# Three pairs instead of four take the plain layer 0 at the front of a four-layer graph network

## The chip, the core and the metric

The kernel runs on one core of a Trainium2 chip. The core has five engines with a queue of instructions each: TensorE (PE in the profile) multiplies matrices into PSUM, VectorE (DVE) and ScalarE (ACT) work on PSUM and SBUF, GpSimd (POOL) on SBUF alone, and SyncE (SP) issues the transfers between the device's memory and SBUF. [...] The metric is the device time of one execution in microseconds; less is better.

## The reference

The input x holds 128 graphs of 64 nodes with 512 features, all with one 64x64 adjacency matrix. Four layers follow, and each ends in `x = layernorm(x + layer(x))`:

- Layer 0: `deg * (x Wi^T + b) + adj (x Wj^T)`, with Wi and Wj the halves of one 512x1024 weight. The kernel applies the graph first, since the graph works on nodes and the weight on features: it forms deg*x and adj*x and multiplies both by their half, 1024 features into 512.
- Layer 1: graph attention with four heads of 512x512, elu, an output attention with a 2048x512 weight, elu, a feed-forward part of two 512x512 weights with relu, and a layernorm of its own with gamma and beta.
- Layers 2 and 3: graph attention with one 512x512 weight each.

All is float32.

## The kernel before

**Tiling.** Two graphs fill the 128 partitions of a tile; two tiles (T = 2) are a pair, of 256 rows. There are NP = 32 pairs, and each goes through the stages `stage_first` (layer 0), `stage_scores` and `stage_heads` (layer 1's attention and its heads), `stage_project` (the output weight), and `stage_late` (output attention, feed-forward, layers 2 and 3). The last pair has `stage_last` and `stage_tile` in place of `stage_late`.

**Two forms of layer 0.** Both begin with the aggregation: PE multiplies x by `aggr` into `axp`, ACT copies that to `ax`, and POOL adds the bias times the degree, `degb`, to x (lines 896 to 912). After that, pairs p >= AHEAD go through `strassen` (line 685): the product of 2x2 blocks is made from seven block products instead of eight. POOL makes sums of `ax` blocks (tiles `s2`, `s3`; in the profile `s`), and the weight's blocks and their differences come ready made from the device's memory, seven parts of 512 KB for every pair (`part_from`, line 613; `ws_w` and `ws_w_T` in the profile, through a ring of four buffers that the output weight's parts share). The products go to the PSUM tiles `stx` and `sty`, and DVE adds them to x. Pairs p < AHEAD take plain products instead, at the front of the program, since the prepared parts are not there yet (lines 914 to 926):

```python
if p < AHEAD:
    ps = psum.tile([P, D], FP, tag="b", name=f"l0_{p}_{t}")
    for k in range(KC):
        with nc.together():
            for s in range(2):
                nc.tensor.matmul(
                    ps, lhsT=ax[:, s, t, k, :], rhs=w0[s][:, k, :],
                    ...
```

A plain tile has eight matmuls of 512 columns. Its PSUM tile is `l` in the profile, where each float32 matmul shows as two records. The last factor of the aggregation also depends on AHEAD (line 905): for Strassen the second tile's `aggr` holds the sum of two blocks.

**The weight's place.** The plain weight `w0` has no buffers of its own. Line 448 puts its halves into the two buffers of the tag `ys`, and `stage_scores` writes its aggregated rows `y` to the same tag (line 976):

```python
w0 = [unit.tile([P, KC, D], FP, tag="ys", bufs=2, name=f"w0_{s}") for s in range(2)]
y = unit.tile([P, KC, 2, T, P], FP, tag="ys", bufs=2, name=f"ys_{p}_{q}")
```

**The front.** The x of pairs below AHEAD is loaded before the weights of the heads (line 541). Then DVE takes 32 dot products of head weights with attention vectors (`score_weights`, line 508, tile `wa_h`). Pairs 0 and 1 get their attention scores from PE: transposes `x1Tp`, products `fp`, then on DVE `over`, on PE `bc`, on DVE a chain of softmax steps that ends in `e`, on PE the transposes `pt`, on ACT the copies `aT`, on PE the aggregation `yp`, and on ACT the copies to `ys`. From `ys` the first head products `sty_h` and `stx_h` start. Other pairs get their scores from DVE's dots with rows of weights (`rows<-d_h`), after which PE turns them (`f2p`). `stage_stream` (line 580) loads every other weight in blocks, has POOL form the differences and stores all to the device's memory, from which `part_from` reads.

**The order.** The stages are generators. A queue in time units (`start`, lines 1303 to 1340; a turn, TURN, is 107) says in which sequence they note their steps: a pair p < AHEAD starts its layer 0 at 0.2 p - 1.2 turns, every other pair at p - 1.1 turns; the scores of p start at p - 0.5, its projection at p + 0.6, its late stage at p + 1.42. The number of a step in that sequence is its rank. `play` (line 327) adds to the rank a shift by kind of step, from the table LATER. A kind is the engine's two first letters and the name of the tile that is written, `te:hidp` for PE's `hidp`. The suffix /S holds for the first 11% of the steps, /E for the last 7%:

```python
when = "S" if i < 0.11 * n else "E" if i > 0.93 * n else "M"
s.rank += LATER.get(s.kind, 0) + LATER.get(f"{s.kind}/{when}", 0)
```

`order` (line 229) then plays the program through with assumed durations (`cost`, line 353). Whenever an engine is free, it takes the ready step of the lowest rank. A step that follows another engine's is ready WAIT + SLACK later, and SLACK for steps behind PE is 0.8. The engines' queues hold the steps in the order found, so every instruction of the program carries the line of the call in `play`, 336. Names of tiles, and not lines, tell the groups of the profile apart.

Of the kernel before, what the change touches and what calls it, by code (L numbers as in the profile page):

```python
# [28 lines left out]
NWS = 4  # L29
NWK = 6  # L30
UNITS = 3
AHEAD = 4

# [4 lines left out]

WAIT = 0.152
NEAR = 150
SLACK = {"tensor": 0.8, "sync": 0.4}

LATER = {
    "gp:never/S": -100, "gp:rs_i": -60, "gp:s_o/S": -20, "gp:ys/E": -40, "sc:aT": -100,
    "sc:aTg/S": 20, "sc:elu/S": -40, "sc:hT": 120, "sc:oT": 60, "sc:who": -80, "sc:xT": -200,  # L50
    "sc:xT/S": -180, "sc:ys/S": 132, "sy:beta/S": -12, "sy:raw_w": 180, "te:fp/S": -20,
    "te:hidp/E": -40, "te:hidp/S": 28, "te:l": 29, "te:l/S": 69, "te:pt": -28, "te:pt/E": 200,
    "ve:e": -29, "ve:e/S": 40, "ve:f_o/S": -120, "ve:hT": 100, "ve:has": 200, "ve:mv": -100,
    "ve:mv/E": 100, "ve:mx": -20, "ve:o": -140, "ve:r": -40, "ve:r/E": 40, "ve:sh": 10,
    "ve:sm": -80, "ve:st": -13,
}


# [105 lines left out]
class Plan:  # L164
# [64 lines left out]
    def order(self):  # L229
# [21 lines left out]
        def late(s, e):  # L251
            return 0.0 if s.engine == e else WAIT + SLACK.get(s.engine, 0.3)

# [120 lines left out]
def gnn_stack_kernel(  # L374
# [43 lines left out]
    def load_x(p):  # L418
        t = xp.tile([P, T, D], FP, tag="x", name=f"x_{p}")
        nc.sync.dma_start(out=t, in_=x[ts(p, T * P), :].rearrange("(t p) d -> p t d", p=P))  # L420
        return t
# [118 lines left out]

    for p in range(1, AHEAD):
        xs[p] = load_x(p)
# [344 lines left out]
    def stage_first(p):  # L887

        if p not in xs:
            xs[p] = load_x(p)  # L890
            yield 0.3 * TURN

        ax = unit.tile([P, 2, T, KC, P], FP, tag="ax", name=f"ax_{p}")
        for t in range(T):
            x = xs[p][:, t, :]
            ps = [
                psum.tile([P, KC, 2, N], FP, tag="b", name=f"axp_{p}_{t}_{b}")
                for b in range(2)
            ]
            with nc.together():  # L900
                for c in range(KC):
                    for b in range(2):
                        nc.tensor.matmul(
                            ps[b][:, c, :, :], lhsT=x[ts(b, N), ts(c, P)],
                            rhs=aggr[ts(b, N), 0 if p < AHEAD else t, :, :], start=True, stop=True,
                        )
            with nc.soon():
                for b in range(2):
                    nc.scalar.copy(
                        ax[:, :, t, :, ts(b, N)], ps[b].rearrange("p c s i -> p s c i")  # L910
                    )
            nc.gpsimd.tensor_tensor(x, x, degb, ALU.add)
            yield 3.0
# [7 lines that stand above are left out]
                                start=(k == 0 and s == 0), stop=(k == KC - 1 and s == 1),  # L921
                            )
                    if k == 1:
                        yield 4.0
                nc.vector.tensor_tensor(x, ps, x, ALU.add)
                normalize(x, f"0_{p}_{t}")
                yield 4.0
        if p >= AHEAD:
            A = lambda k, t: ax[:, k, t, :, :]
            yield from strassen(  # L930
                A, part_from("w0", p), sums(A, KC, nc.gpsimd), xs[p], KC, f"0_{p}", 3.0,
                whole=lambda t: normalize(xs[p][:, t, :], f"0_{p}_{t}"),
            )
        first.add(p)
        yield 0.0
# [367 lines left out]
    def start(at, order, stage):  # L1303
        heapq.heappush(queue, (at, order, stage))

    for p in range(NP):
        if p < AHEAD:
            start(TURN * (0.2 * p - 1.2), 10 * p + 4, stage_first(p))
# [84 lines left out]
```

## Time and profile before

| | us |
|---|---|
| median of three runs | 3310.98 (3309.94 to 3311.04) |
| the profiled execution | 3313.95 |
| its span, first to last instruction | 3312.2 |
| PE busy | 3265.2 (99%) |
| DVE busy | 2374.4 (72%) |
| POOL busy | 1724.0 (52%) |
| ACT busy | 1364.6 (41%) |
| mean granted clock of TensorE | 0.994 |
| DMA | 726.08 MB, 219 GB/s |

The profile shows one execution. Busy time adds up an engine's instructions; PE's are pipelined, so a record lasts longer than the distance to the next. The granted clock is the share of TensorE's full clock that the chip gave it in a stretch. A group of the profile reads "line engine operation, tile written <- tiles read, forms, count", and a bracket or a last column gives the idle time ahead of it with the instruction that ended it. The timeline counts from the start of the span.

### The profile page before, as it was taken

The page shows a single profiled execution, that of the slowest core. Times are in us where ns is not written, and L with a number is a line of the kernel's source. Part 1 is how long each engine was busy: PE and PEld are TensorE (multiplying, and loading weights), DVE is VectorE, ACT ScalarE, POOL GpSimd, SP SyncE. Part 2 cuts the span into 40 slices and gives each one's busy share as a digit, 9 for nine tenths or more (in the row PEclk, how much of TensorE's full clock was granted, in tenths as well). Part 3 has the DMA queues.
Part 4 walks back from the last instruction along what each step waited for, and adds up shares of the span by engine and source line. Part 5 has one row for each costly group of instructions (what it writes and reads, how often), then busy time and mean ns, then how long its engine had stood idle before and what let it go on. Part 6 is the DMA issues. An engine that isn't in the chain of part 4 may idle for free.

```text
span 3312.2 us, 60000 instructions
## 1 busy us (share of the span) xinstructions
PE 3265.2 (99%) x21268; PEld 2881.8 (87%) x21268; DVE 2374.4 (72%) x5668; ACT 1364.6 (41%) x3226; POOL 1724.0 (52%) x1860
## 2 busy tenths in 40 slices
PE   8999999999999999999999999999999999999997
PEld 4888888898988989989889988888889899898885
DVE  5467767777777777777777777777777767777766
ACT  2434344343444434444443443434444344343442
POOL 6745445554555555455454555645554455554442
PEclk9999999999999999999999999999999999999998
DMA  8956666767667676667766667676666766667652
GB/s 303 338 177 215 221 203 215 234 208 237 211 210 233 213 247 197 200 230 221 242 204 220 212 217 236 214 226 208 214 233 208 246 201 202 229 216 238 227 183 77
DMA packets 306584, 726.08 MB, mean 219 GB/s; under 512 B 34240, under 2 KB 43504, under 8 KB 306288
## 3 DMA queue, kind: packets, MB, share of 16 engines
q1 hardware_dynamic: 306288, 722.26, 67.1%
q8 instruction: 171, 2.80, 0.3%
q14 instruction: 125, 1.02, 0.1%
HBM read 688.69 MB, written 33.44 MB: 218 GB/s over the span
## 4 chain that ended last, share of the span: by engine, by line
PE 91%; DVE 4%; DMA 3%; POOL 1%; issue 1%; ACT 0%; SPq 0%; POOLq 0%; DVEq 0%; ACTq 0%
PE stx_h L336 13%; PE stx_o L336 13%; PE stx L336 12%; PE sty_h L336 10%; PE sty_o L336 9%; PE sty L336 9%; PE hidp L336 7%; PE yp L336 4%; PE gp L336 3%; PE stx_y L336 3%; PE sty_y L336 2%; PE axp L336 2%; PE l L336 1%; PE op L336 1%; PE oTp L336 1%; DMA d_f<-f 1%
## 5 line engine op out<-in xcount | busy, mean ns | idle before, releaser
L336 DVE CUSTOM_DVE_ANT_0 j<-x,rows 128x512 bf16<-128x512 f32 x736 | 584.1, 794 | 94.3 <-DMA rows<-d_h 75.6
L336 PE MATMUL stx_h<-ys,wh 128*128 128x128 f32 x3072 | 403.8, 275 | 0.7 <-DVE hT L336 0.7
L336 PEld LDWEIGHTS stx_h<-ys,wh 128*128 128x128 f32 x3072 | 381.1, 192 | 22.3 <-DVE sh L336 5.7
L336 POOL TENSOR_SCALAR rs<-mv 128x1 f32<-128x1 f32 x256 | 104.1, 407 | 406.2 <-DVE mv L336 392.2
L336 ACT COPY hT<-stx_h 128x256 f32<-128x256 f32 x384 | 143.0, 372 | 384.6 <-PE stx_h L336 378.6
L336 ACT ACTIVATE x<-x,sh,rs 128x512 f32<-128x512 f32 x256 | 207.2, 813 | 223.6 <-DVE sh L336 221.0
L336 PE MATMUL sty_h<-ys,wh 128*128 128x128 f32 x2048 | 273.8, 277 | 0.0
L336 PEld LDWEIGHTS sty_h<-ys,wh 128*128 128x128 f32 x2048 | 254.4, 192 | 9.0 <-issue 0.5
L336 PE MATMUL stx_o<-ws_wo_T,s_o 128*128 128x256 f32 x1024 | 246.0, 383 | 0.5 <-ACT who L336 0.5
L336 DVE TENSOR_TENSOR x<-stx,x 128x256 f32<-128x256 f32 x360 | 150.8, 420 | 132.1 <-PE stx L336 131.0
L336 PE MATMUL sty_o<-ws_wo,hT 128*128 128x256 f32 x1024 | 243.2, 380 | 0.1
L336 PE MATMUL hidp<-oT,w 128*128 128x256 f32 (+1 forms) x1056 | 228.9, 373 | 0.0
L336 PEld LDWEIGHTS hidp<-oT,w 128*128 128x128 f32 x1056 | 194.0, 190 | 24.9 <-ACT oT L336 0.2
L336 PEld LDWEIGHTS stx_o<-ws_wo_T,s_o 128*128 128x128 f32 x1024 | 190.2, 191 | 28.4 <-ACT who L336 2.1
L336 PEld LDWEIGHTS sty_o<-ws_wo,hT 128*128 128x128 f32 x1024 | 190.8, 191 | 25.6 <-issue 1.1
L336 DVE SCALAR_TENSOR_TENSOR hT<-elu,hT 128x512 f32<-128x512 f32 x256 | 174.9, 684 | 43.3 <-ACT elu L336 41.3
L336 POOL TENSOR_TENSOR ys<-ys,t 128x256 f32<-128x256 f32 x128 | 102.9, 814 | 189.8 <-PE sty_h L336 189.4
L336 ACT ACTIVATE elu<-hT 128x512 f32<-128x512 f32 x256 | 153.0, 599 | 108.7 <-DVE hT L336 104.6
L336 POOL TENSOR_TENSOR rs<-rs,mhalf 128x1 f32<-128x1 f32 x256 | 173.4, 677 | 21.1
L336 DVE BATCH_NORM_STATS2 st<-x 128x6 f32<-128x512 f32 x256 | 176.5, 689 | 5.1
L336 DVE TENSOR_TENSOR hT<-sty_h,hT 128x256 f32<-128x256 f32 x256 | 107.2, 420 | 81.2 <-PE sty_h L336 69.3
L336 ACT COPY ys<-yp 128x512 f32<-128x512 f32 x256 | 132.2, 602 | 78.4 <-PE yp L336 71.7
(205 smaller groups left out, 7629.3 us busy)
## 6 DMA issues: line engine op xcount, KB each, us to landing
ws_wo_T<-d_wo_T SPq DMA_DIRECT2D x256, 512.0 KB, 3.9
ws_wo<-d_wo SPq DMA_DIRECT2D x192, 512.0 KB, 5.3
ws_W_T<-d_W_T SPq DMA_DIRECT2D x248, 256.0 KB, 4.2
rows<-d_h SPq DMA_DIRECT2D x240, 256.0 KB, 4.7
ws_w_T<-d_w_T SPq DMA_DIRECT2D x112, 512.0 KB, 4.9
ws_W<-d_W SPq DMA_DIRECT2D x186, 256.0 KB, 4.1
ws_w<-d_w SPq DMA_DIRECT2D x84, 512.0 KB, 5.2
rows<-d SPq DMA_DIRECT2D x128, 256.0 KB, 4.3
```

The costliest lines, as they stand in the source:

```text
L336: getattr(getattr(self.tc.nc, s.engine), name)(*map(real, args), **{k: real(v) for k, v in kw.items()})
```

## The change

AHEAD goes from 4 to 3. Pair 3 thus loses its place at the front: its x is not loaded ahead of the head weights, its aggregation uses the other `aggr` for the second tile, its layer 0 starts at 1.9 turns instead of -0.6, and it is made by `strassen` with streamed parts instead of by plain products. The table LATER is replaced by another, and SLACK behind PE goes from 0.8 to 0.799. No other line changes.

```diff
-AHEAD = 4
+AHEAD = 3
...
-SLACK = {"tensor": 0.8, "sync": 0.4}
+SLACK = {"tensor": 0.799, "sync": 0.4}
...
 LATER = {
-    "gp:never/S": -100, "gp:rs_i": -60, "gp:s_o/S": -20, "gp:ys/E": -40, "sc:aT": -100,
-    "sc:aTg/S": 20, "sc:elu/S": -40, "sc:hT": 120, "sc:oT": 60, "sc:who": -80, "sc:xT": -200,
-    "sc:xT/S": -180, "sc:ys/S": 132, "sy:beta/S": -12, "sy:raw_w": 180, "te:fp/S": -20,
-    "te:hidp/E": -40, "te:hidp/S": 28, "te:l": 29, "te:l/S": 69, "te:pt": -28, "te:pt/E": 200,
-    "ve:e": -29, "ve:e/S": 40, "ve:f_o/S": -120, "ve:hT": 100, "ve:has": 200, "ve:mv": -100,
-    "ve:mv/E": 100, "ve:mx": -20, "ve:o": -140, "ve:r": -40, "ve:r/E": 40, "ve:sh": 10,
-    "ve:sm": -80, "ve:st": -13,
+    "gp:gT/S": -200, "gp:hid": 60, "gp:hid/S": 80, "gp:ident": -80, "gp:mhalf": -60,
+    "gp:raw_W": 20, "gp:raw_w/S": -40, "gp:raw_wo/S": -40, "gp:ys/E": -60, "sc:aT": -280,
+    "sc:elu/S": -180, "sc:o": 20, "sc:o/S": -40, "sc:who": -100, "sc:ys/S": 140,
+    "te:bc/E": -120, "te:bc/S": 120, "te:fp/S": -120, "te:hidp": -3, "te:hidp/E": 34,
+    "te:hidp/S": 120, "te:l": 40, "te:l/S": 51, "te:pt": -28, "te:pt/E": 220, "te:stx_o/S": -36,
+    "te:sty/E": -60, "te:sty_y": -40, "te:sty_y/S": 80, "te:xTp/S": 60, "ve:e": -160,
+    "ve:f_o/S": -120, "ve:hT": 200, "ve:has": 360, "ve:mv": -160, "ve:o": -360, "ve:r": -180,
+    "ve:sh": 10, "ve:sm": -80, "ve:st": -13,
 }
```

## The prediction

> **What bounds the kernel now.** I read the page first: busy shares, then the slices.
>
> ```profile
> PE 3265.2 (99%) x21268; PEld 2881.8 (87%) x21268; DVE 2374.4 (72%) x5668; ACT 1364.6 (41%) x3226; POOL 1724.0 (52%) x1860
> ...
> PE   8999999999999999999999999999999999999997
> ```
>
> TensorE (PE) is the bound; only the first and last slice fall below nine tenths. Next, busy time by stretches, cut where the timeline of PE changes character (columns: stretch, length, busy us of PE, its weight loads, DVE, ACT, POOL, then granted clock, DMA share, GB/s).
>
> ```profile
> 14.20:68.00 53.80, 51.87 (x220) 26.61 (x218) 34.95 (x87) 13.68 (x25) 37.08 (x35) 1.00 0.89 314
> 68.00:92.00 24.00, 23.32 (x123) 13.77 (x124) 11.69 (x19) 9.82 (x23) 18.39 (x15) 0.93 0.94 337
> ...
> 180.00:232.00 52.00, 46.37 (x248) 37.86 (x247) 33.35 (x78) 17.47 (x42) 17.22 (x19) 0.90 0.72 226
> 232.00:330.00 98.00, 96.74 (x681) 87.11 (x681) 72.45 (x169) 43.05 (x106) 60.33 (x61) 1.00 0.59 186
> 330.00:3200.00 2870.00, 2864.01 (x18920) 2565.40 (x18919) 2099.73 (x4993) 1203.34 (x2848) 1489.75 (x1611) 1.00 0.68 220
> ...
> 3240.00:3312.00 72.00, 52.28 (x184) 33.87 (x183) 44.76 (x136) 20.34 (x58) 16.90 (x32) 0.83 0.20 62
> ```
>
> From 330 to 3200 us PE idles 6 us of 2870: there only less PE work helps. What an order can win lies in 180 to 232 (5.6 idle, clock 0.90) and after 3240. Third, the timeline of PE (start, length, what; brackets: idle before it, and what ended that).
>
> ```profile
> 68.68 1.03 PE L336 MATMUL x1Tp<-ident,x 128*128 128x128 f32 x4 [1.99 <-ACT ax L336]
> 69.51 8.38 PE L336 MATMUL l<-w,ax 128*128 128x512 f32 x16
> 77.73 0.60 PE L336 MATMUL pt<-ident,e 128*128 128x128 f32 x4
> 78.17 3.60 PE L336 MATMUL l<-w,ax 128*128 128x512 f32 x8
> 81.60 1.85 PE L336 MATMUL fp<-wa_h,x1T 128*128 128x8 f32 x16
> 83.38 2.95 PE L336 MATMUL yp<-aT,x 64*128 64x128 f32 x48
> 86.26 3.70 PE L336 MATMUL l<-w,ax 128*128 128x512 f32 x8
> ...
> 91.94 1.05 PE L336 MATMUL sty_h<-ys,wh 128*128 128x128 f32 x8
> ```
>
> `l` is the plain product, 16 records a tile, 128 in all. These last 32 are two tiles, by their number and place pair 3's; the first head product follows at 91.94. The timeline of ACT shows what they hold up:
>
> ```profile
> 89.14 4.01 ACT L336 COPY ys<-yp 128x512 f32<-128x512 f32 x8 [4.72 <-PE l L336]
> ```
>
> The two `ys` buffers held the plain weights w0. The copy of the finished `yp` waits 4.72 us for an `l`, the last reader of w0. So the heads start only when every front pair's plain product is done.
>
> **What the Trainium skill says.** "TensorE: Matmul & The Clock Gate", Part 1, says that PE falls to half clock after an idle window of about 3.4 us and returns after a busy one. The trace agrees on rate and length: 68.8 to 72.2, 184.9 to 191.7 and 225.8 to 229.2 us each show a granted clock of 0.50. It differs on the trigger: gaps of 1.99 and 2.53 us precede the first and third. So an idle gap here costs itself plus about 1.7 us for each such window. The same page, Back-to-back issue gap, prices 512 columns at 216 ns. Here eight `l` records take 3.43 us (78.17 to 81.60), 429 ns each, and 256 columns 216: the measurement decides. "SBUF — State Buffer", SBUF: two separate sides, calls the port pair of VectorE and GpSimd an exclusive lock; the trace agrees (a 128x1 `sh` took 2.29 us at 65.02 beside a long POOL subtraction, 0.15 at 25.73).
>
> **The change part by part.**
> *PE work.* Out: 32 records of 429 ns, 13.7 us. In: seven products of four matmuls, two records each, 56 x 216 ns = 12.1. The aggregation `axp` stays (two groups of 1.16, 2.3 us), so pair 3's layer 0 later costs 14.4. Saving alone: 1.6.
> *The front.* Removed are pair 3's `axp` (2.3, the sixteens at 46 and 52 us) and the `l` stretches 8.2, 3.4 and 3.6: 17.6 us, a half-clock loss of 1.7 among them. That shortens the time to the first head only as far as the attention chain of pair 0 follows. I walk that chain. Scores end at 61.6, `over` at 63.0. `bc` runs at 65.23 behind eight `l` of pair 2 (2.1 lost); `e` starts 2.7 later than `bc` allows, because DVE does pair 2's `sh`, add and statistics; `e` is finished at 74.9, but `pt` waits for the sixteen `l` until 77.7 (2.7); `yp` runs at 83.4 where `aT` was there at 80.4 (3.0); the `ys` copies start at 89.1 where the first `yp` groups were done by 84.7 (4.4). The last three, 10.1, are pair 3's and go. The load of x_3 (512 KB) leaves a queue at 390 GB/s ahead of W_heads: 1.3 us. Sum 11.4. The first two (4.8) are pair 2's and depend on the new places; I take half. So the first head comes 13.8 earlier, 78.1 us, against 14.4 paid later: **+0.6**. Bounds: only the `ys` wait goes, 4.4, giving +10.0; all 17.6 goes, giving -3.2.
> *92 to 330 us.* Bracketed idle there: 1.50+1.06+0.70+1.55+0.29+0.46+2.53+0.37+0.89 = 9.35. The half-clock windows 184.9 to 191.7 and 225.8 to 229.2 hold 9.7 us of busy PE, half lost: 4.9. Together 14.2. The waits are on `hT`, `e_1o`, `aT_1o`, `who`: latencies of few chains, with no layer-0 product in sight. Pair 4's `axp` comes at 301.9, its products at 332 to 358. Pair 3's come a turn (104 us) earlier, about 198 to 254, inside this stretch, and `ve:e`, `ve:r`, `ve:o`, `sc:aT` move the very steps that PE waits for ahead. I take half: **-7.1** (bounds -14.2, and +3 for one new gap with its window).
> *Tail.* Brackets from 3200 on add to 15.9, half clock to 8.0 (16.0 busy in three windows), PE's last record ends 7 before the span: 31. In the last seven per cent of the steps `ve:mv` goes from 0 to -160, `ve:r` from 0 to -180, both on the serial chain of norms and attentions; `te:hidp` from -40 to +31. I take 5%: **-1.5** (bounds -9 and +9).
> *At nothing.* Pair 3's extra DVE: one 128x512 add of 0.69 and five of 0.42 for two of 0.69, +1.4; POOL: three `s`/`ax` sums of 1.27, +3.8; the weight loads of PE, 56 for 32 at 190 ns. They hide beneath PE (in 180 to 232 DVE is 64% busy, POOL 33%); uncovered, 5.2 together. Pair 3's `degb` adds, `rs`, `ax` copies and normalization leave a front where POOL is 77% busy (18.4 of 24) for one that is emptier: no price, it is in the chain above. DMA: x_3 moves on SP behind the stream stores, and seven w0 parts of 512 KB join, 3.7 MB or 17 us at 220 GB/s, with a DMA share of 0.6 to 0.7 around them. Each takes one of the four `ws` buffers, which the `wo` parts use, so its issue waits on SP for their last reader. Behind it stand the `rows` of pair 2's and 3's scores, on which DVE's dots wait 4.0 us between 180 and 232 already; PE sees that only if `f2p` of pair 3 (290.4 before, 36 after pair 3's products) gets late. The w0 stream's stores are issued by 127, some 70 before use. SLACK 0.799 and the other places have 6 us of idle to work on between 330 and 3200: 0 (-2 to +3).
> *Sum.* +0.6-7.1-1.5 = -8.0. Against the profiled execution (3313.95, span 3312.2, 1.75 around it): 3305.9. Its median of runs lies 2.97 lower, at 3310.98: **3303 us**.
>
> **The rivals.**
> *The front chain becomes the bound (slower).* Place: fp to the first head, 60 to 92 us. DVE is the reason: 32 score dots end at 57.9 whatever pair 3 does, and PE would have only pair 1's transposes as cover. If just the 4.4 is gained, the front is +10.0, and PE idle for over 10 us runs the next 6.8 at half clock, +3.4: 3324. It decides once the first head comes after 84.1 (a gain under 7.8) with nothing won later. For it: POOL is 18.4 of 24 busy there and stretches DVE. Against: the three waits counted away are visibly `l`'s.
> *The gaps only move (same).* Starved chains at 180 to 232 come earlier with the heads and keep their latencies; pair 3's products arrive after them. Then +0.6 and the tail zero: 3311.6. For it: the waits are latencies, not missing work.
> *The tail opens (slower).* Two more gaps like the one of 3.49 us at 3283 with windows of 6.8, 2 x (3.5+3.4) = 13.8, less half of the gain in the middle and the rest: 3319.
> That pair 3 is pulled to the front again is excluded: its parts are stored too late.
>
> **How the numbers follow.** Chances: forecast 0.48 (own range 3294 to 3304), same 0.17, front chain 0.27, tail 0.08. A difference of 0.2%, 6.6 us, is about what a measurement of this kernel can tell from no change; so faster 0.48, same 0.17, slower 0.35. The low end is +0.6 in front, the whole 14.2 of the middle and 3 of the tail, 3294; 0.05 lies below. The high end of 3322 is a front of +11; some 0.13 of the front rival and 0.02 of the tail lie above.
>
> **What would show it.** No `l` after about 75 us and 96 in all; 56 more `stx`/`sty` with `ax`; the first `sty_h` near 78 (after 84: the front rival); bracketed idle of PE from there to 330 at half of 9.4 and one half-clock window fewer; span from 3200 to the end of the same shape less 1 or 2 us. Wrong if idle between the last `l` and the first head exceeds 8 us, or if the tail's idle grows past 20.

## The result, and the profile after

The changed kernel takes 3316.12 us (median of 15 runs, 3312.87 to 3321.87) against 3310.29 (15 runs, 3304.11 to 3316.41) of the kernel before beside it: a ratio of 1.0016 with a 95% interval of 1.0009 to 1.0022. It is slower by 0.16%, some 5 us, where 8 us less were forecast. Its profiled execution took 3314.58 us with a span of 3312.8, 0.6 longer than the span before; a second profile of it has a span of 3318.3. The profiled execution of the kernel before, 3313.95, lies 3.7 above its median, so the first pair of profiles shows less of a difference than the medians do.

The page after, busy shares and slices:

```profile
PE 3260.1 (98%) x21292; PEld 2887.1 (87%) x21292; DVE 2393.4 (72%) x5672; ACT 1361.8 (41%) x3226; POOL 1726.1 (52%) x1863
...
PE   7999999999999999999999999999999999999997
```

PE is busy for 5 us less, but its first slice has gone from 8 to 7. The same stretches as before (length, busy us of PE, its weight loads, DVE, ACT, POOL; granted clock, DMA share, GB/s):

```profile
14.20:68.00 53.80, 47.90 (x187) 24.46 (x187) 33.07 (x87) 14.25 (x27) 36.11 (x32) 1.00 0.95 344
68.00:92.00 24.00, 16.73 (x125) 14.66 (x126) 13.03 (x19) 9.36 (x21) 19.50 (x16) 0.64 1.01 371
...
180.00:232.00 52.00, 51.49 (x336) 45.32 (x334) 30.33 (x61) 18.20 (x40) 30.12 (x31) 0.95 0.64 198
232.00:330.00 98.00, 97.28 (x619) 86.15 (x619) 71.45 (x176) 39.34 (x93) 42.78 (x51) 1.00 0.71 226
330.00:3200.00 2870.00, 2864.76 (x18963) 2569.24 (x18962) 2123.43 (x4995) 1201.67 (x2855) 1498.72 (x1618) 1.00 0.68 220
3240.00:3312.00 72.00, 51.70 (x190) 32.94 (x190) 44.64 (x136) 20.84 (x59) 17.05 (x32) 0.85 0.21 62
```

Between 180 and 232 us PE's idle time went from 5.6 to 0.5 and its clock from 0.90 to 0.95: the gain in the middle came. But between 68 and 92 PE now idles 7.3 instead of 0.7, at a clock of 0.64 instead of 0.93. The timeline of PE there:

```profile
56.56 1.85 PE L337 MATMUL fp<-wa_h,x1T 128*128 128x8 f32 x16
58.26 3.68 PE L337 MATMUL l<-w,ax 128*128 128x512 f32 x8
...
62.76 1.02 PE L337 MATMUL bc<-over,bones 128*128 128x512 f32 x2
68.16 3.16 PE L337 MATMUL fp<-wa_h,x1T 128*128 128x8 f32 x16 [4.38 <-ACT x1T L337]
77.59 2.08 PE L337 MATMUL bc<-over,bones 128*128 128x512 f32 x2 [6.27 <-DVE over L337]
...
81.36 6.31 PE L337 MATMUL yp<-aT,x 64*128 64x128 f32 x64 [0.84 <-ACT aT L337]
87.59 1.16 PE L337 MATMUL sty_h<-ys,wh 128*128 128x128 f32 x8
```

The plain products end at 61.9. `bc` of pair 0 runs soon after, at 62.76, and from there PE has only the attention chain: it idles 4.38 and 6.27, and the second `fp` and `bc` run at half clock (3.16 and 2.08 us for 1.85 and 1.02). The first head product comes at 87.59, 4.3 earlier than before and 9.5 later than forecast. The timeline of DVE shows where pair 0's softmax stands:

```profile
63.43 0.18 DVE L337 BATCH_NORM_AGGREGATE mv<-st 128x2 f32<-128x6 f32 x1
71.43 0.69 DVE L337 TENSOR_TENSOR e<-bc,f 128x512 f32<-128x512 f32 x1 [7.81 <-PE fp L337]
72.04 0.55 DVE L337 SCALAR_TENSOR_TENSOR sh<-mv,rs 128x1 f32<-128x1 f32 x1
...
76.35 1.18 DVE L337 TENSOR_TENSOR over<-f,ident 128x512 f32<-128x512 f32 x1
```

Its inputs `bc` and `f` are there by 63.8, yet `e` waits 7.81 us for the `fp` of the next pair. What it waits for is not data but a buffer: pair 1's transposed rows `x1T` lie in the buffers of the tags `dg` and `e`, and `fp`, which ends at 71.3, is their last reader. The timeline of ACT shows why that `fp` is late in turn:

```profile
63.82 0.25 ACT L337 COPY wat_h<-wap_h 32x128 f32<-32x128 f32 x1 [0.22 <-PE bc L337]
67.53 0.58 ACT L337 COPY x1T<-x1Tp 128x512 f32<-128x512 f32 x1 [3.45 <-DMA d_h<-wat_h]
```

The other `x1T` takes the buffer of `dg`, in which `wat_h` lies until its store has landed. In the kernel before, pair 1's `x1T` came at 74.1 and 78.4, after pair 0's first `e`. These lines of its timelines of DVE and ACT show the order:

```profile
68.77 0.66 DVE L336 TENSOR_TENSOR e<-bc,f 128x512 f32<-128x512 f32 x1
...
74.09 0.56 ACT L336 COPY x1T<-x1Tp 128x512 f32<-128x512 f32 x1
```

**An account by stretches.** For the runs below I price every record of PE at its mean distance to the next between 400 and 3050 us (`l`, which does not occur there, at 429 ns), and call what a stretch takes beyond the sum its loss: idle time, half clock and late starts together. "Head" is the first `sty_h`. The first 14 us (losses of 3.0 to 4.7) and the 5 before PE's first record are left out. The two profiles of the changed kernel, after and after_again, differ by up to 2.4 in a column, so single differences of that size say nothing.

| | head at | loss 14 to head | head to 180 | 180 to 330 | 330 to 3000 | 3000 to 3200 | 3200 to end |
|---|---|---|---|---|---|---|---|
| before | 91.9 | 6.4 | 3.9 | 13.2 | 2.8 | -1.0 | 34.1 |
| after | 87.6 | 18.6 | 6.9 | 2.6 | -3.6 | 3.2 | 34.4 |
| after_again | 89.1 | 19.9 | 5.0 | 4.8 | -1.6 | 2.6 | 36.8 |
| e1_ahead_only | 85.4 | 15.7 | 9.9 | 10.5 | 0.4 | 6.5 | 36.1 |
| e2_places_only | 103.0 | 19.2 | 6.3 | 11.0 | 13.9 | 0.1 | 33.5 |
| e3_own_buffers | 79.5 | 10.6 | 18.7 | 5.5 | 0.5 | 3.4 | 34.7 |
| e3b_own_buffers_before | 90.0 | 4.9 | 6.6 | 11.1 | 4.4 | -0.6 | 32.9 |
| e6_own_late | 81.4 | 11.4 | 14.8 | 12.0 | 2.8 | 2.9 | 35.3 |
| e7_late_before | 90.1 | 4.4 | 13.4 | 17.0 | 1.1 | -0.7 | 32.0 |
| e8_cover | 90.8 | 10.8 | 7.2 | 5.7 | 17.5 | 3.4 | 34.4 |
| e9_same_order_own | 88.4 | 19.2 | 5.7 | 4.3 | -0.1 | 2.6 | 32.8 |
| e10_pair4_early | 90.5 | 4.6 | 4.8 | 8.8 | 7.8 | 8.3 | 32.6 |
| e11_rs_first | 86.6 | 18.0 | 7.8 | 3.8 | 0.0 | 3.0 | 32.4 |
| e12_rs_first_own | 82.1 | 13.7 | 10.7 | 1.4 | -1.1 | 3.7 | 35.3 |

The sum of the prices is 3243.7 with four pairs in front and 3242.3 with three, 3256.0 for e8_cover. So of before against after: work -1.4, front +12.2, head to 330 us -7.6, the long middle -6.4, the stretch before 3200 +4.2, tail +0.3, the first 14 us -0.4. They add to 0.9, rounding included, where the spans differ by 0.6.

### The profile page after: what moved, and what is told of

The parts are those of the page before. It is cut to its first block, busy times and chain, and to the rows that moved or that the text cites. A ratio compares the mean times of both kernels' runs of the same rounds, so it can differ in the third digit from the quotient of the medians.

```text
span 3312.8 us, 60061 instructions
## 1 busy us (share of the span) xinstructions
PE 3260.1 (98%) x21292; PEld 2887.1 (87%) x21292; DVE 2393.4 (72%) x5672; ACT 1361.8 (41%) x3226; POOL 1726.1 (52%) x1863
## 3 DMA queue, kind: packets, MB, share of 16 engines
q14 instruction: 125, 1.02, 0.1%
## 4 chain that ended last, share of the span: by engine, by line
PE 91%; DMA 4%; DVE 2%; POOL 1%; SPq 1%; issue 1%; ACT 0%; POOLq 0%; DVEq 0%; ACTq 0%
PE stx_o L337 13%; PE stx_h L337 13%; PE stx L337 12%; PE sty_h L337 10%; PE sty_o L337 10%; PE sty L337 9%; PE hidp L337 6%; PE yp L337 4%; PE gp L337 3%; PE stx_y L337 3%; PE sty_y L337 2%; PE axp L337 2%; PE op L337 1%; PE oTp L337 1%; SPq L337 1%
## 5 line engine op out<-in xcount | busy, mean ns | idle before, releaser
L337 POOL TENSOR_TENSOR s<-gT 128x256 f32<-128x256 f32 x62 | 49.5, 798 | 270.3 <-DVE gT L337 258.4
L337 ACT COPY ax<-axp 128x512 f32<-128x512 f32 x128 | 68.5, 589 | 281.6 <-PE axp L337 277.8
```

Source lines behind the costliest of these rows:

```text
L337: getattr(getattr(self.tc.nc, s.engine), name)(*map(real, args), **{k: real(v) for k, v in kw.items()})
```

## The experiments

Each was run beside the kernel before on the same chip.

**The two parts alone.** e1_ahead_only is the kernel before with

```diff
-AHEAD = 4
+AHEAD = 3
```

> AHEAD = 3 alone; table LATER and SLACK as before. Loss is the time of a stretch less PE's records in it, priced at their distances in the steady part: from 14 us to the first head product 6.4 before and 18.6 after, from there to 330 us 17.2 before and 9.5 after. Theory A (with three pairs in front, pair 1's transposed rows get the buffers 'e' and 'dg' ahead of pair 0's softmax, whatever the places): front loss 15 to 20, first head at 85 to 90 us. Theory C (the new places delay pair 0): front loss under 10, first head at 76 to 80. For the middle: if pair 3's seven-product layer 0 is the filler, loss to 330 us under 11; if the new places did it, about 17. A time of 3312 to 3320 under A with the filler, 3308 to 3312 under C.

e2_places_only keeps `AHEAD = 4` and takes the new LATER and SLACK:

> The new LATER and SLACK 0.799 alone; AHEAD stays 4. Theory A: front loss as before, 6 to 9, first head at 91 to 94 us. Theory C: front loss 15 or more, first head after 97. Middle: filler theory 15 to 19 of loss to 330 us, places theory about 9. A time of 3308 to 3314 under A with the filler theory, 3302 to 3306 under A with the places theory, 3318 or more under C.

Measured: 3332.39 us against 3307.93, a ratio of 1.0073 (1.006 to 1.0087), and 3344.31, 1.011 (1.0096 to 1.0124). Each part alone is worse than both together, and neither has the gain in the middle: head to 330 us loses 20.4 and 17.3, before 17.1, after 9.5. Two parts that cost 0.7% and 1.1% alone cost 0.16% together, so the places and the number of pairs can't be priced apart. Both times lie far above what was expected under theory A. In front, e2 gives the figures of theory C: with four pairs there, the new places alone delay pair 0, at waits on `ax` and `e`. e1 gives those of theory A, but not its mechanism: pair 1's `fp` is through at 66.9, before pair 0's `bc` ends at 68.9, so the shared buffer holds nothing up there. What e1 does have is the hole of the changed kernel ahead of pair 1's `bc`, whose `over` stands behind pair 0's softmax in DVE's queue; this hole needs no new places:

```profile
75.79 2.08 PE L336 MATMUL bc<-over,bones 128*128 128x512 f32 x2 [6.88 <-DVE over L336]
```

**The shared buffers.** e3_own_buffers is the changed kernel, e3b_own_buffers_before the kernel before, with

```diff
-xT = unit.tile([P, KC, P], FP, tag=("dg", "e")[t], name=f"x1T_{p}_{t}")
+xT = unit.tile([P, KC, P], FP, tag="s3", bufs=2, name=f"x1T_{p}_{t}")
```

> The changed kernel, with the transposed rows x1T of pairs 0 and 1 in the two buffers of tag s3, which stand empty then, instead of 'dg' and 'e'. Theory A: DVE's e of pair 0 no longer waits for fp of pair 1, and x1T no longer for the landing of d_h; first head at 79 to 82 us instead of 87.6, front loss 9 to 13, half clock there at most 7 us instead of 17.1; time 6 to 9 under the changed kernel's, 3307 to 3310. Theory B (the chain of scores and softmax is that long by itself): first head at 86 to 88, time as the changed kernel's, 3314 to 3318.

> The kernel before with the same move of x1T to s3: a control. There pair 0's softmax had the buffer first, and PE is covered by pair 3's plain products. Theory A and B: no change, first head within 1.5 us of 91.9, time within 3 us of before. More than 4 us faster would say that the shared buffers cost the kernel before as well.

Measured: 3328.94 against 3307.93, 1.0068 (1.0055 to 1.0081), and 3311.21, 1.0009 (1.0002 to 1.0015). In e3 the first head comes at 79.5, as early as I had forecast for the change, and the loss ahead of it falls by 8.0. But by the ratios the whole is 0.3 to 0.5% slower than the changed kernel (1.0016 in one set of runs, 1.0037 in another), where a gain of 6 to 9 us was expected. The control comes out 3 us slower, at the edge of what was expected. The timeline of PE shows where the next idle time stands:

```profile
121.26 3.35 PE L337 MATMUL sty_o<-ws_wo,hT 128*128 128x256 f32 x8 [5.91 <-DMA ws_wo<-d_wo]
132.25 1.99 PE L337 MATMUL sty_o<-ws_wo_T,hT 128*128 128x256 f32 x8 [2.52 <-DMA ws_wo_T<-d_wo_T]
...
183.31 0.44 PE L337 MATMUL pt_1o<-ident,e_1o 128*128 128x128 f32 x1 [5.05 <-DVE e_1o L337]
```

The heads are done earlier, and the output weight's parts are not: they are issued at 117.4 in this run and land after. Head to 180 loses 18.7. But with the new buffers the planner found another order, so this run alone can't separate the two.

**That gate moved.** e6_own_late is e3 with the stream that prepares w0 later, e7_late_before the kernel before with the same edit:

```diff
-start(0.6 * TURN, 0, stage_stream(W0T, "w0"))
+start(1.2 * TURN, 0, stage_stream(W0T, "w0"))
```

> x1T in the buffers s3 as in e3_own_buffers, and the stream that prepares w0 noted at 1.2 turns instead of 0.6, so that it no longer goes through the four ws buffers ahead of pair 0's output weights. Ring theory (in e3 the 8 us won in front were lost again where sty_o waited 5.9 and 2.5 us for ws_wo, because the w0 stream held the ring): ws_wo is issued before 110 us instead of 117.4, the loss from the first head to 180 us falls from 18.7 to under 9, first head still at 79 to 81; time 8 to 15 under e3's 3328.9, 3314 to 3321. Bandwidth theory (the transfers are simply not done by then): ws_wo lands no earlier than 118 us, loss 15 to 20, time 3324 to 3332.

> The kernel before with the w0 stream at 1.2 turns instead of 0.6, nothing else. Its chain of waits runs through that stream to stx_o at 134 us. Ring theory: ws_wo issued before 115 us instead of 124.4, the waits of 1.5 and 1.1 us at 126.6 and 133.1 go, loss from the first head to 180 us 1 to 3 instead of 3.9; time 3305 to 3310, since little is idle there. Bandwidth theory: no change, 3308 to 3313. More than 6 us slower would say that the stream at its new place delays something later.

Measured: 3332.36 against 3306.13, 1.0074 (1.0061 to 1.0086), and 3325.2, 1.0055 (1.0043 to 1.0067). Both times missed. The edit costs the kernel before as well (head to 330 loses 30.4 for 17.1). In e6 the first part `ws_wo` is issued at 97.8, before the 110 expected, and PE's wait at 121 us is gone; but up to 180 us it still loses 14.8, where under 9 was expected, since its timeline has two other waits:

```profile
156.62 3.75 PE L337 MATMUL stx_o<-ws_wo_T,s_o 128*128 128x256 f32 x8 [8.57 <-POOL s_o L337]
188.38 0.45 PE L337 MATMUL pt_1o<-ident,e_1o 128*128 128x128 f32 x1 [6.13 <-DVE e_1o L337]
```

The idle time has moved and not gone. As each of these orders was found anew, they don't show that the new waits stood behind the old one all along.

**More cover.** e8_cover is the changed kernel with a plain product's worth of needless work for each tile of pair 2, 13.7 us of PE in all:

```diff
+if p == AHEAD - 1:
+    ps = psum.tile([P, D], FP, tag="b", name=f"l0_{p}_{t + T}")
+    for k in range(KC):
+        with nc.together():
+            for s in range(2):
+                nc.tensor.matmul(
+                    ps, lhsT=ax[:, s, t, k, :], rhs=w1_sb[:, k, :],
+                    ...
```

> The changed kernel with 16 needless plain products in front, as many as pair 3's were: layer 0 of pair 2 multiplies its aggregation by w1 into two PSUM tiles that nobody reads. It adds 13.7 us of PE work and leaves nothing out. Cover theory (the front waits on other engines and pair 3's plain products stood there for nothing): the first head comes at 87 to 93 us all the same, front loss falls from 18.6 to 5 to 10 with the needless work counted as work, time 0 to +5 on the changed kernel. Work theory (PE work is what the front costs): first head at 98 to 102 us, time +10 to +14.

Beside it the changed kernel ran again:

> The changed kernel unaltered, on the chip of the three runs below: 3 to 7 us over the kernel before. Front loss (14 us to the first head product, time less priced PE work) 18 to 19, first head at 87 to 88 us, as in its first profile, if these are the program's and not one execution's.

Measured: 3345.83 and 3319.74 against 3306.13, ratios of 1.0121 (1.0108 to 1.0134) and 1.0037 (1.0023 to 1.005). The first head comes at 90.8, where 87.6 and 89.1 stood without the needless work: 13.7 us more of PE's work moved it by 2 to 3, and the loss ahead of it fell from 18.6 and 19.9 to 10.8. That fits the cover theory, but it doesn't show that the chain takes its time anyway, since the chain isn't the same. PE's timeline of e8:

```profile
75.54 1.02 PE L337 MATMUL bc<-over,bones 128*128 128x512 f32 x2
...
90.81 1.16 PE L337 MATMUL sty_h<-ys,wh 128*128 128x128 f32 x8
```

The new order has the needless products ahead of pair 0's `bc`, which runs 12.8 later than in the changed kernel. From there to the head it takes 15.3 us instead of 24.8, for in this order pair 1's `x1T` come after pair 0's `e`, and pair 2's `sh` are done before it. The late start and the shorter chain nearly cancel. The time as a whole missed: with the order found anew, 17.5 us of loss appeared between 330 and 3000, far from the edit.

**The same order.** To be rid of that, e9_same_order_own plans with the old buffers and makes the real tiles with the new ones. Each engine's order is that of the changed kernel:

```diff
-self.made = self.pool.real.tile(self.shape, self.dtype, **self.args)
+args = self.args
+if args.get("name", "").startswith("x1T_"):
+    args = {**args, "tag": "s3", "bufs": 2}
+self.made = self.pool.real.tile(self.shape, self.dtype, **args)
```

> The changed kernel with every engine's instructions in the very same order (the order is found as before, and only the buffers that x1T of pairs 0 and 1 really get are changed, from 'dg' and 'e' to s3). So nothing is planned anew. Theory A1 (the shared buffers alone are the loss in front, and what is won there stays won): first head at 79 to 82 us, time 6 to 9 under the changed kernel, which ran at 3319.7 beside a kernel before at 3306.1, so 5 to 8 over the kernel before. Theory A2 (behind that gate stands a second, the prepared output weights at 121 us, so idle of PE moves there and is not removed): first head at 79 to 82, loss from 14 us to the first head 9 to 12 instead of 18.6 to 19.9, loss from there to 180 us 11 to 15 instead of 5 to 7, time within 3 us of the changed kernel. Theory B (the chain itself is that long): first head at 86 to 89.

Measured: 3316.54 (3312.89 to 3321.92) against 3311.32, 1.0019 (1.001 to 1.0028), the changed kernel's time; the first head at 88.4, where theory B had it. The buffer's wait is gone and nothing is gained, but not because the chain itself is that long. The timeline of DVE says why:

```profile
64.26 0.69 DVE L340 TENSOR_TENSOR e<-bc,f 128x512 f32<-128x512 f32 x1 [0.21 <-PE bc L340]
71.56 0.16 DVE L340 SCALAR_TENSOR_TENSOR sh<-mv,rs 128x1 f32<-128x1 f32 x1 [6.60 <-POOL rs L340]
71.63 0.69 DVE L340 SCALAR_TENSOR_TENSOR bc<-e 128x512 f32<-128x512 f32 x1
```

`e` starts 7.2 us earlier. Next in DVE's queue is pair 2's `sh`, which waits 6.60 for `rs`, and pair 0's softmax stands behind it. The timeline of POOL of the same run has `rs` behind three long subtractions for the output weight:

```profile
63.50 7.18 POOL L340 TENSOR_TENSOR raw_wo<-raw_wo,raw_wo 128x1024 f32<-128x1024 f32 x3
70.65 0.22 POOL L340 TENSOR_SCALAR rs<-mv 128x1 f32<-128x1 f32 x1
```

In the changed kernel the two `rs` (each of two records) stand behind the same subtractions and end at 70.5 and 71.3, about when the buffer comes free (71.3). Its POOL timeline:

```profile
62.49 7.18 POOL L337 TENSOR_TENSOR raw_wo<-raw_wo,raw_wo 128x1024 f32<-128x1024 f32 x3
...
70.78 0.56 POOL L337 TENSOR_TENSOR rs<-rs,mhalf 128x1 f32<-128x1 f32 x1
```

So two gates of nearly one length stand side by side, of which the waits named only one. In the kernel before, POOL's timeline has the first of them ahead of those subtractions:

```profile
64.11 0.22 POOL L336 TENSOR_SCALAR rs<-mv 128x1 f32<-128x1 f32 x1
...
64.95 4.79 POOL L336 TENSOR_TENSOR raw_wo<-raw_wo,raw_wo 128x1024 f32<-128x1024 f32 x2
```

The new LATER ranks `raw_wo` 40 earlier at the start (`gp:raw_wo/S`), which the old one doesn't. With the old table e1 too has an `rs` ahead of the three subtractions and one between them (62.9 and 66.1); with the new one e2 too runs the three in a row. That may point to this entry, but no run changes it alone.

**Both gates.** e11_rs_first keeps the changed kernel's order and buffers, but takes the `rs` steps of pair 2 forward in POOL's queue: those of the first tile ahead of all three subtractions and three `wh` differences before them, those of the second tile ahead of the last two subtractions. e12_rs_first_own has the buffers of e9 besides.

```diff
-for s in self.order():
+steps = self.order()
+first = [
+    s for s in steps if s.engine == "gpsimd"
+    and any(t.args.get("name", "").startswith("rs_0_2_") for t in s.uses)
+]
+for f in first:
+    steps.remove(f)
+    past = f.after | f.behind
+    i = 1 + max(i for i, s in enumerate(steps) if s in past)
+    steps.insert(i, f)
+for s in steps:
```

> The changed kernel in its own order on every engine but POOL, where the four small `rs` steps of pair 2 are taken ahead of the three long subtractions of output-weight blocks (7.2 us) that stood before them. The shared buffers of `x1T` and `e` stay. Theory of two gates side by side: DVE is free for pair 0's softmax at about 64, but the first `e` still finds its buffer taken by pair 1's `x1T` until pair 1's `fp` has read it, so `e` stays near 71.4 us, the first head product near 87.6 (86 to 89), and the time within 3 us of the changed kernel's, 3313 to 3319. Rival, that `rs` alone was the cause: `e` at about 65, first head near 81, time 3306 to 3310.

> The same, with buffers of their own for the `x1T` tiles as well; the order of every engine is that of the run before. Both theories: `e` at about 64 to 66, first head product at 80 to 83, loss between 14 us and the first head down from 18.6 to about 8 to 12. Theory of the next gate: the output weight's parts `ws_wo` land no earlier than 121 to 123 us, since the ring of four buffers and the stores of the w0 stream set them, so PE waits for them (or for the chains at 150 to 183) and gets 5 to 8 us of new idle and half clock there; the time stays within 3 us of the changed kernel's, 3313 to 3319. Rival, that the front was the one thing wrong and my sum would have held: the 6 to 8 us stay won, 3306 to 3310, a ratio to the kernel before of 0.998 to 1.000.

Measured: 3316.47 (3313.49 to 3320.1) and 3317.63 (3309.42 to 3326.38) against 3308.06, ratios of 1.0028 (1.0018 to 1.0038) and 1.0029 (1.002 to 1.0038). In e11 `e` stays at 71.64 and the head at 86.6: either gate alone holds the chain, as e9 showed for the other. With both gone the first head comes at 82.1, 5.5 earlier than in the changed kernel. DVE's timeline of e12:

```profile
63.46 0.69 DVE L350 TENSOR_TENSOR e<-bc,f 128x512 f32<-128x512 f32 x1 [0.21 <-PE bc L350]
64.07 1.54 DVE L350 SCALAR_TENSOR_TENSOR sh<-mv,rs 128x1 f32<-128x1 f32 x1
...
66.98 2.29 DVE L350 SCALAR_TENSOR_TENSOR sh<-mv,rs 128x1 f32<-128x1 f32 x1 [0.76 <-POOL rs L350]
```

`e` is 8.0 earlier, but the two `sh` now run beside POOL's subtractions and take 3.8 us for 1.8, ahead of pair 0's softmax. In e3, where the order was found anew, neither gate stands on the chain: DVE's timeline has `e` at once and pair 2's `sh` behind the softmax, and the head came at 79.5.

```profile
63.67 0.69 DVE L337 TENSOR_TENSOR e<-bc,f 128x512 f32<-128x512 f32 x1 [0.21 <-PE bc L337]
...
71.01 0.16 DVE L337 SCALAR_TENSOR_TENSOR sh<-mv,rs 128x1 f32<-128x1 f32 x1 [1.36 <-POOL rs L337]
```

PE's timeline of e12:

```profile
72.28 2.08 PE L350 MATMUL bc<-over,bones 128*128 128x512 f32 x2 [6.08 <-DVE over L350]
...
88.89 1.16 PE L350 MATMUL sty_h<-t,wh 128*128 128x128 f32 x8 [2.08 <-POOL t L350]
...
121.04 1.97 PE L350 MATMUL stx_o<-ws_wo,hT 128*128 128x256 f32 x8 [1.02 <-DMA ws_wo<-d_wo]
```

PE still idles 6.08 ahead of pair 1's `bc`, since its `over` stands behind pair 0's softmax in DVE's queue. The loss ahead of the head falls by 4.9 against the changed kernel, to 13.7 where 8 to 12 was expected, and 3.8 come back by 180: at `t`, which POOL makes behind the subtractions, at `ws_wo`, and at a half-clock window of 3.4 us. The first output product on `ws_wo` stands at 121.04; in the changed kernel, with a head 5.5 later, it stands at 121.5. PE's order is the same in both, so the same work lies ahead of it, and 5.0 of the 5.5 are gone by then. The time is the changed kernel's; the interval leaves room for some 3 us either way. That is what the theory of the next gate gives, though no single wait takes the whole: I had put 5 to 8 us on `ws_wo` and the chains after it, and `ws_wo` shows 1.02.

**The middle by itself.** e10_pair4_early is the kernel before with one Strassen layer 0 a turn earlier, as the change has it with pair 3's:

```diff
-start(TURN * (p - 1.1), 10 * p + 4, stage_first(p))
+start(TURN * (p - (2.1 if p == AHEAD else 1.1)), 10 * p + 4, stage_first(p))
```

> The kernel before (four plain pairs in front, old places) with one more edit: layer 0 of pair 4, the first of seven products, is noted at 1.9 turns instead of 2.9, where pair 3's stands in the changed kernel. It asks whether the two gains can be had together, pair 3's plain cover in front and a seven-product layer 0 as filler behind. If the filler is what emptied the stretch from 180 to 330 us of idle time: axp of pair 4 at about 205 to 215 us, loss from 180 to 330 us 3 to 8 instead of 13.2, loss in front 5 to 8 as before, time 4 to 9 under the kernel before. If the places did it, or if the new plan opens gaps further on: loss there 10 or more, time within 3 us of the kernel before or slower.

Measured: 3323.43 against 3311.32, 1.0041 (1.0028 to 1.0053). The front is that of before (loss 4.6) and 180 to 330 loses 8.8 for 13.2, so a product in the middle seems to fill part of it; e3b, which has none there, shows 11.1. But 330 to 3000 loses 5.0 more and 3000 to 3200 9.3 more, in an order found anew with a table made for another program. No version that I ran beats the kernel before.

## Why the prediction was wrong

**PE work** (-1.6): right, -1.4 by the prices. The 32 `l` records are gone, the 56 `stx` and `sty` came. The 216 ns for 512 columns that the prediction quotes from the Trainium skill ("TensorE: Matmul & The Clock Gate", Back-to-back issue gap) is the figure there for an isolated matmul, not for a stream; no price rests on it.

**The front** (+0.6): this step failed. It had two parts. The 14.4 us paid later were right. The 13.8 gained came from adding up the waits for `l` that were visible on the chain, 10.1 of them called pair 3's, and treating the chain behind them as free to follow. It moved 4.3 (2.8 in the second profile), so the term is 14.4 - 4.3 = +10.1. The waits for `l` did vanish: `bc` runs 2.5 earlier than before. But the queues were filled anew, and the order found puts two waits on the chain for which the sum had nothing: pair 1's `x1T` in the buffer of pair 0's `e`, and pair 2's `rs` behind POOL's subtractions, on which DVE's queue stood. e9 and e11 show that either alone holds the head; without both it comes at 82.1 in the same order (e12) and at 79.5 in another (e3), near the 78.1 of the forecast.

The term also took for granted that what the head gains stays gained. No run bears that out: by 121 us e12 has only 0.5 left of its 5.5, and e3, whose loss ahead of the head is 8.0 smaller than the changed kernel's, loses 14.7 more from there to 330.

Two items of the sum were off besides. Of the 3.0 at `yp`, some 1.8 were pair 1's `fp` (81.60 to 83.45) and not pair 3's `l`. And my half of 4.8 us for pair 2's steps on DVE named their place, but not that they would cost instead of give.

**The rival of the front** came nearer in size: +10.0 there and 3.4 for half clock, with a head after 84.1, where +10.1 and +11.6 were measured with the half clock in them; it was given 0.27. It named DVE busy with other work and PE without cover. PE was without cover; DVE, though, was idle for 7.81 us, waiting. It also took it that nothing would be won later, so its 3324 is 8 us above the median measured, my 3303 13 below. What came is its front with the middle of my forecast.

**92 to 330 us** (-7.1): right in size and place, though the half that I took was a guess, so that it came out so close is in part luck. Head to 330 lost 9.5 instead of 17.1, -7.6; bracketed idle time of PE from 180 to 330 went from 6.8 to 1.2 us (from 92 on, 9.4 to 4.0), and one half-clock window is gone. Pair 3's aggregation stands at 206.3 and its products at 229.9 to 257, where about 198 to 254 was forecast for both, these two lines of the changed kernel's PE timeline being the aggregation and the first of them:

```profile
206.34 1.16 PE L337 MATMUL axp<-aggr,x 64*128 64x128 f32 x16
...
229.87 1.89 PE L337 MATMUL sty<-ws_w,ax 128*128 128x256 f32 x8
```

That the products as such are the cause is supported only in part: e10 won 4.4 with a like product, e1 has the products and won 2.7 between 180 and 330, which is hardly more than two profiles of one program differ by. The part of the new places is not shown.

**Tail** (-1.5): missed, +0.3 and +2.7 in two profiles. Its bracketed idle time went from 15.9 to 17.3.

**330 to 3200** (0, -2 to +3): -2.2 (-6.4 up to 3000, +4.2 after) and -0.8. The sum of what was measured, +10.1-7.6-2.2+0.3, is +0.6, the difference of the two spans (the work is inside the front's 14.4). The second profile gives +6.1, with a front of +11.6. The medians lie 5.8 us apart, and single executions of the changed kernel up to 9.0. Which stretch makes the rest of the difference between medians stays open with two profiles.

**The checks named.** No `l` after 75 and 96 in all: so. First head near 78, after 84 for the rival: the rival. Idle time between the last `l` and the head above 8 us as the sign of being wrong: it is 4.38+6.27+0.84 = 11.5.

## What to carry to other kernels

A wait on the chain tells what ends it last, not what would end it next. Before counting it as gained, look up when the buffer that the next step writes comes free and what stands ahead of it in its engine's queue and in its releaser's queue; here two gates ended within a microsecond of each other, and opening either alone gave nothing.

Taking away work that looks like the bound of a start-up need not bring forward the chain that ran beside it. And with a planner that finds the order anew, compare stretches, or freeze the order and change one thing: an edit in the front moved the loss between 330 and 3000 us by up to 21 us.

## What the runs showed of the hardware

Outside the tail, half clock came only in lengths of 3.41, 6.83, 10.24, 13.65 and 17.07 us, and once of 20.48 (after_again), in the traces of all runs. Within a trace the starts lie on one grid of such steps: 68.81 and 184.86 in the kernel before are 34 of them apart. In the changed kernel one of 17.07 us follows the gap of 4.38 and holds on while PE works: from 69 to 85 us it is busy 8.9 of 16. The stretch of that trace (columns as above):

```profile
69.00:85.00 16.00, 8.89 (x45) 6.94 (x47) 11.44 (x16) 4.27 (x10) 13.39 (x12) 0.50 1.01 363
```

The Trainium skill ("TensorE: Matmul & The Clock Gate", Part 1: The HAM clock gate) tells of a free-running activity window of 4096 cycles, about 3.4 us; steps of 3.41 us agree. I had priced one window per gap; here a chain of small products with gaps between them stayed at half clock for five, and for six in the second profile.
